# Sampling tiles of unequal width: eleven tiles of 12 columns become ten of 11, 13, 14 and 11

## The chip, the cores and the metric

The kernel runs on one core of a Trainium2 chip. A core has a matrix engine (TensorE, in the profile PE, its weight loads PEld), a vector engine (VectorE, DVE), an engine for activations and copies (ScalarE, ACT), GpSimd (POOL) and SyncE (SP), whose queue issues most DMA transfers. The metric is device time in microseconds; the median of several runs is compared.

## The reference

The input x is (2, 256, 128, 128): batch, channels, rows, columns. After a group norm, a first layer runs three branches with distances (dilations) 1, 9 and 12. Each branch computes offsets by a 3x3 convolution, samples the image at the nine shifted positions with bilinear weights, and sums the samples with one weight for each channel and tap:

```
off = conv(x, w_off, pad, dil)                   # 18 planes: (y, x) of nine taps
py = yy - pad + ky*dil + off[:, :, 0];  px = xx - pad + kx*dil + off[:, :, 1]
y  = einsum('bckhw,ck->bchw', bilinear(x, py, px), w)
out_branch = gelu(layernorm_over_channels(y))
```

The branches and a 1x1 convolution are added and normalised, a two-layer MLP with gelu follows, then a residual, a layer norm and the addition of x. A second layer adds a 3x3 convolution with weights quantised to three values. What is computed in the sampling: `sum over the four neighbours of (1-|dy|)(1-|dx|) * x`, for every tap and pixel.

## The kernel before

The program has three phases. **Phase one** (`phase_a`, up to about 0.9 ms) normalises x, writes it pixel by pixel, channels last, into a padded table in DRAM (`tables`), and computes the offsets. From these, `make_hats` writes tent functions ("hats") to DRAM: for each tap, and each of the rows and columns that a tile of source pixels has, the weight `max(0, 1 - |distance|)` that a sampling position gives to it. `offsets` also records in `reach` how far offsets go; positions that the tiles do not cover are listed by `missing` and mended singly.

**Phase two** (`sample_near`) is the sampling, and the change is in it. The padded image is cut into blocks of `RI` = 2 rows and `CI` = 12 columns; a tile of source pixels adds a margin of `REACH` = 2 on each side, so it has `TR` = 6 rows and `TC` = 16 columns, `PX` = 96 pixels, one for each partition. There are `NT` = 11 such blocks across the 132 padded columns. The outer loop goes over units: image (2), row pair `Rt` (66), branch (3). For a unit:

- `load_tiles` (L1301), once for a row pair and one row pair ahead, loads the eleven source tiles `xs`, pixel on partition, 256 channels of 4 bytes; 18 buffers turn.
- `load_hats` (L1327) loads `hy` and `hx` for each of the three tap rows: 96 partitions of 3 KB each, 2 rows by 3 taps by 128 positions. The source pattern of hy repeats the 6 row hats for each column, that of hx the 16 column hats for each row. Three buffers of each turn, so one unit fills them.
- `build` (L1347, VectorE) multiplies hy and hx into `A`, two of which turn; the positions are shifted so that a block's samples lie together.
- `sample` (L1448, TensorE) multiplies tile and A for one half of the channels: a column is one tap of one position, so a full block has 9 taps x 2 rows x 12 = 216 columns. Block 0 goes alone into a PSUM bank, then two blocks to a bank. ScalarE copies the banks to `ev` (L1460, L1468), six copies for a channel half.
- `accumulate` (L1409, VectorE; first tap L1391, ScalarE) adds the nine taps, each times its channel weight, into ring buffers of finished rows.

`columns` says which taps of a block fall inside the image. With blocks of 12 the first and last block drop three of nine taps at distance 12 and none at distance 9. A program instruction for float32 is two MATMUL records in the trace. The order on the compute engines is the program's (`pin`); between the pieces, `tail.advance` runs the rest of the network (norms, gelu, MLP) on finished groups of four rows. DMA issues are placed in SP's queue by a planner, each behind its semaphore waits, and the queue is in order: one that waits holds those behind it. `prepare(u + 2)` builds A two units ahead and asks for the hats of the unit after that.

**Phase three** (from about 5.7 ms) is the second layer's convolution.

Of the kernel before, what the change touches and what calls it, by code (L numbers as in the profile page):

```python
# [9 lines left out]
F32 = mybir.dt.float32  # L10
# [4 lines left out]
ALU = mybir.AluOpType  # L15
# [4 lines left out]
P = 128  # L20
# [20 lines left out]
RI, CI = 2, 12  # L41
TR, TC = RI + 2 * REACH, CI + 2 * REACH
NT = -(-(W + 2 * REACH) // CI)
PX = TR * TC
WT = NT * CI + 2 * REACH
AO = 12
WA = 28 + W
NH = TR + TC + 2
# [8 lines left out]
XCLS = (0, 1, 3, 9, 11)  # L57
# [3 lines left out]
SPAN = (REACH + (RI - 1) / 2, REACH + (CI - 1) / 2)  # L61
NPAT = RI + len(XCLS) + 1

# [8 lines left out]
def conv_preact_kernel(ctx: ExitStack, tc: tile.TileContext, t: dict, out: bass.AP):  # L72
# [248 lines left out]
    def phase_a(b, pool, psum, k, beside, todo):  # L321
# [53 lines left out]
        def offsets(G):  # L375
# [49 lines left out]
            nc.vector.tensor_tensor(rest, offs, k["mid"], ALU.subtract)  # L425
            planes = rest.rearrange("p r (b c k) -> p c r b k", c=2, k=9)
# [76 lines left out]
    def missing(psum, pool, tabs):  # L503
# [15 lines left out]
        nc.vector.tensor_scalar(V, reach[:, 0], SPAN[0], None, ALU.is_gt)  # L519
        nc.vector.scalar_tensor_tensor(V, reach[:, 1], SPAN[1], V, ALU.is_gt, ALU.max)  # L520
# [19 lines left out]
        for j in range(8):  # L540
            one = pool.tile([P, ROWS], F32, name="one", tag="one", bufs=3)
            nc.vector.tensor_scalar(one, slot, rank[:, j : j + 1], None, ALU.is_equal)
            nc.tensor.matmul(
                pl[0:ROWS, 0 : 2 + 2 * NTAP], lhsT=one, rhs=what[:, j, :], start=j == 0, stop=j == 7
            )
# [35 lines left out]
        nc.vector.tensor_copy(base[:, 1], pl[0:R_, 2 : 2 + 2 * NTAP])  # L581
        by, mid = base[:, :, 0:NTAP], base[:, :, NTAP:]
# [23 lines left out]
        for d in range(2):  # L606
# [3 lines left out]
            for c in range(2):  # L610
                nc.vector.tensor_scalar(cd[:, c], cd[:, c], SPAN[c] ** 2, None, ALU.is_le)
# [79 lines left out]
    def list_tables(pool):  # L691
        sizes = (NB * H + ROWS + P, NTAP, 3 * NTAP, 2 * NTAP, 8 * (2 + 2 * NTAP), NB * H)
# [15 lines left out]
    with ExitStack() as actx:  # L708
        psum = actx.enter_context(tc.tile_pool(name="ps_a", bufs=1, space=PSUM))

        def gps():
# [9 lines left out]
            "mid": ap.tile([P, ZG, NOFF], F32, name="mid"),  # L721
            "hatw": ap.tile([P, 2, NTAP * NH], BF16, name="hatw"),
# [10 lines left out]
        for b in range(NB):  # L733
# [12 lines left out]
            if b == 0:  # L746
# [3 lines left out]
                nc.sync.dma_start(k["mid"], t["mid"])  # L750
                hatw = ap.tile([P, 2, NTAP * NH], F32, name="hatw32", tag="xt", bufs=3)
# [505 lines left out]
    def sample_near(pool, psum, k):  # L1257
# [33 lines left out]
        def load_tiles(b, Rt):  # L1291

            xts[b, Rt] = []
            for T in range(NT):
                xt = pool.tile([PX, C], F32, name="xs", tag="xs", bufs=18)
                src = bass.AP(
                    table[b].tensor,
                    table[b].offset + (Rt * RI * WT + T * CI) * C,
                    [[C, TC], [WT * C, TR], [1, C]],
                )  # L1300
                nc.sync.dma_start(xt, src)  # L1301
# [109 lines left out]
        def columns(br, T):  # L1411

            dil = DILS[br]
            kept = [
                i
                for i, s in enumerate((-dil, 0, dil))
                if max(0, REACH + s) < (T + 1) * CI
                and T * CI < min(W + 2 * REACH, W + REACH + s)
            ]
            return kept[0] * RI, (kept[-1] + 1) * RI  # L1420

        def sample(u, c):
# [11 lines left out]
            n = (y1 - y0) * 3 * RI * CI  # L1434
            ev = pool.tile([P, 9 * RI, NT * CI], F32, name="ev", tag="ev", bufs=3)
            evv = ev.rearrange("p (y m) w -> p y m w", y=3)
            for T in range(-1, NT, 2):
                if T == 2 * ((NT + 1) // 4) - 1:
                    tail.advance()
                ts = range(max(T, 0), T + 2)  # L1440
                pm = k["pm"][tail.banks % len(k["pm"])]
                tail.banks += 1
                pv = pm[:, :, 0:n].rearrange("p j (y m w) -> p j y m w", y=y1 - y0, w=CI)
                reach = [columns(br, t) for t in ts]
                for j, t in enumerate(ts):
                    m0, m1 = reach[j]
                    pin(
                        nc.tensor.matmul(  # L1448
                            pv[:, j, :, m0:m1, :],
                            lhsT=xts[b, Rt][t][:, c * P : (c + 1) * P],  # L1450
                            rhs=A[:, y0:y1, m0:m1, AO + t * CI : AO + (t + 1) * CI],
# [4 lines left out]
                m0, m1 = min(r[0] for r in reach), max(r[1] for r in reach)  # L1456
                if m1 - m0 == 3 * RI:
# [512 lines left out]
```

## Time and profile before

| | |
|---|---|
| median of 3 runs | 6653.83 us (6651.51 to 6657.11) |
| profiled execution, its own time | 6654.54 us |
| its span, first to last instruction | 6652.5 us |
| mean granted TensorE clock | 0.971 |
| moved by DMA | 1360.48 MB, mean 205 GB/s |

The page gives busy time for each engine, then groups of instructions by source line: `L1448 PE MATMUL pm<-A,xs` is the sampling product of line 1448, with its count, its busy time in all and its mean duration in ns, and after the second bar the time for which the engine stood idle just before it and what ended the waiting. The chain is the work that ended last, followed back from the end; a share of it is time that the work set. In the waits, "SPq L1327 <- DVE A L1347" is a DMA issue of line 1327 that waited for the VectorE instruction that writes A.

### The profile page before, as it was taken

What the parts mean: (1) busy time and instruction counts of PE and PEld (TensorE: products, weight loads), DVE (VectorE), ACT (ScalarE), POOL (GpSimd) and SP (SyncE); (2) the same over time, 40 slices, a digit from 0 to 9 for tenths busy, and PEclk for the clock granted to TensorE, in tenths of its full rate; (3) what the DMA queues carried; (4) which work ended last, traced back from release to release, by engine and by line L of the source; (5) the groups of instructions that cost most, each with busy time, mean ns of one, the idle gap of its engine ahead of it and who ended that gap; (6) DMA issues with size and microseconds to landing.
All of it is one profiled execution on the core that took longest, in us unless ns stands there. A gap on an engine that the chain in (4) does not pass through costs nothing.

```text
span 6652.5 us, 100588 instructions
## 1 busy us (share of the span) xinstructions
PE 6295.0 (95%) x32242; PEld 5006.0 (75%) x32242; DVE 5907.6 (89%) x13772; ACT 4194.8 (63%) x8690; POOL 687.1 (10%) x665
## 2 busy tenths in 40 slices
PE   5899978999999999999999999999999999989999
PEld 3455558888888888888888888888888888734444
DVE  7766657999999999999878999999999999689996
ACT  1344436677777777777676777777777777554442
POOL 0000000111111111111110111111111111200000
PEclk9999978999999999999999999999999999989999
DMA  8976657877887777877667877778777787343332
GB/s 285 281 211 196 201 158 208 227 220 218 222 224 217 219 215 222 226 220 210 189 192 199 226 221 218 216 221 229 224 217 220 218 222 207 121 163 132 135 141 90
DMA packets 635794, 1360.48 MB, mean 205 GB/s; under 512 B 109592, under 2 KB 290344, under 8 KB 618736
## 3 DMA queue, kind: packets, MB, share of 16 engines
q1 hardware_dynamic: 617328, 1318.97, 68.8%
q10 hardware_dynamic: 17408, 33.56, 1.6%
q8 instruction: 261, 4.28, 0.3%
q14 instruction: 285, 2.33, 0.1%
q0 software_dynamic: 512, 1.34, 0.1%
HBM read 1087.10 MB, written 266.47 MB: 203 GB/s over the span
## 4 chain that ended last, share of the span: by engine, by line
PE 54%; DVE 28%; DMA 8%; ACT 6%; issue 3%; SPq 1%; POOL 0%; DVEq 0%; ACTq 0%; POOLq 0%
PE pm L1448 23%; DVE ring L1409 12%; PE hp L890 6%; PE pc L1789 6%; PE h L1133 5%; PE pz L364 4%; DVE A L1347 4%; DMA hx<-hats 3%; ACT ev L1460 3%; PE pc L1133 2%; DMA xa<-in_x 2%; ACT v L1111 2%; PE ph L463 2%; PE tp L905 1%; DVE st L1097 1%
## 5 line engine op out<-in xcount | busy, mean ns | idle before, releaser
L1448 PE MATMUL pm<-A,xs 96*128 96x216 f32 (+2 forms) x17424 | 3258.3, 344 | 180.3 <-ACT ev L1460 44.4
L1448 PEld LDWEIGHTS pm<-A,xs 96*128 96x128 f32 x17424 | 3058.0, 195 | 380.0 <-ACT ev L1460 124.2
L1409 DVE SCALAR_TENSOR_TENSOR ring<-ev,defw,ring 128x256 f32<-128x256 f32 (+4 forms) x6372 | 2481.2, 451 | 98.1 <-ACT ev L1460 52.1
L1460 ACT COPY ev<-pm 128x432 f32<-128x432 f32 (+4 forms) x4488 | 1991.9, 483 | 883.2 <-PE pm L1448 702.4
L1347 DVE TENSOR_TENSOR A<-hy,hx 96x768 f32<-96x768 f32 (+1 forms) x1124 | 1010.3, 945 | 180.3 <-DMA hx<-hats 100.2
L1103 POOL TENSOR_TENSOR rs<-rs,mhalf 128x4 f32<-128x4 f32 x320 | 472.5, 1477 | 4223.5 <-DVE rs L1102 3672.0
L1789 PE MATMUL pc<-cring,signs 128*128 128x512 bf16 x3456 | 758.2, 383 | 17.0 <-ACT cring L1706 7.4
L1111 ACT ACTIVATE v<-v,rs 128x256 f32<-128x256 f32 x1280 | 694.2, 594 | 17.0 <-POOL rs L1104 16.8
L1789 PEld LDWEIGHTS <-signs 128*128 128x128 bf16 x3456 | 339.7, 98 | 434.8 <-issue 28.0
L890 PE MATMUL hp<-S,w 128*128 128x512 f32 x1024 | 500.5, 614 | 0.8 <-ACT S L1213 0.8
L364 PE MATMUL pz<-wz,xa 128*128 128x486 f32 x1024 | 463.5, 580 | 28.1 <-DVE zr L371 28.0
L1097 DVE BATCH_NORM_STATS2 st<-v 128x6 f32<-128x256 f32 x1280 | 446.9, 410 | 35.0 <-ACT v L921 35.0
L1133 PE MATMUL h<-w,hT 128*128 128x256 f32 x2048 | 477.1, 379 | 0.0
L1391 ACT ACTIVATE ring<-ev,defw 128x256 f32<-128x256 f32 (+1 forms) x856 | 404.4, 485 | 24.1
L1133 PEld LDWEIGHTS h<-w,hT 128*128 128x128 f32 x2048 | 369.3, 190 | 65.5 <-issue 1.0
L364 PEld LDWEIGHTS pz<-wz,xa 128*128 128x128 f32 x1024 | 189.5, 192 | 193.5 <-issue 126.8
L921 ACT COPY v<-tp 128x512 f32<-128x512 f32 x384 | 207.7, 597 | 183.5 <-PE tp L913 182.7
L1222 ACT ACTIVATE hT<-hp,b 128x512 f32<-128x512 f32 x256 | 176.1, 688 | 222.5 <-PE hp L890 217.3
L890 PEld LDWEIGHTS hp<-S,w 128*128 128x128 f32 x1024 | 198.8, 199 | 141.4 <-issue 126.8
L470 ACT ACTIVATE hb<-ph 96x512 f32<-96x512 f32 (+1 forms) x384 | 209.9, 596 | 145.0 <-PE ph L463 138.6
L1133 PE MATMUL pc<-convw,xn 128*128 128x256 f32 x1024 | 271.5, 394 | 2.5 <-ACT xn L1194 2.5
L371 ACT COPY zr<-pz 128x486 f32<-128x486 f32 x128 | 72.3, 565 | 260.0 <-PE pz L364 257.3
(246 smaller groups left out, 5135.7 us busy)
## 6 DMA issues: line engine op xcount, KB each, us to landing
hy<-hats SPq DMA_DIRECT2D x1112, 288.0 KB
hx<-hats SPq DMA_DIRECT2D x1112, 288.0 KB
xs<-tables SPq DMA_DIRECT2D x1452, 96.0 KB
g12d<-v SPq DMA_DIRECT2D x128, 512.0 KB
other<-g12d SPq DMA_DIRECT2D x128, 512.0 KB
hats<-hb SPq DMA_DIRECT2D x64, 720.0 KB
hats<-hb SPq DMA_DIRECT2D x64, 576.0 KB
xa<-in_x ACTq DMA_DIRECT2D x64, 512.0 KB
```

The source lines that it names most:

```text
L364: nc.tensor.matmul(pz[:, 0:NZ], lhsT=xt[:, c, r, :], rhs=k["wz"][:, c, :], start=c == 0, stop=c == KC - 1,)
L890: nc.tensor.matmul(out, lhsT=w, rhs=v, start=i == 0, stop=i == n - 1)
L1097: pin(nc.vector.bn_stats(st[:, j, :], rows[j]))
L1103: nc.gpsimd.tensor_tensor(rs[:, 0, :], rs[:, 0, :], mhalf[:, 0:n], ALU.pow)
L1111: nc.scalar.activation(row, row, func, scale=rs[:, 0, j : j + 1], bias=rs[:, 1, j : j + 1])
L1133: nc.tensor.matmul(bank[:, j, :], lhsT=v[:, px], rhs=w, start=False, stop=i == len(pairs) - 1,)
L1347: nc.vector.tensor_tensor(dst, hy[:, i0:i1].rearrange("p i t w -> p t i w"), hx[:, i0:i1].rearrange("p i t w -> p t i w"), ALU.mult,)
L1391: pin(nc.scalar.mul(dst, src, w))
L1409: pin(nc.vector.scalar_tensor_tensor(dst, src, w, dst, ALU.mult, ALU.add))
L1448: nc.tensor.matmul(pv[:, j, :, m0:m1, :], lhsT=xts[b, Rt][t][:, c * P : (c + 1) * P], rhs=A[:, y0:y1, m0:m1, AO + t * CI : AO + (t + 1) * CI],
L1460: nc.scalar.copy(dst.rearrange("p m (t j) -> p t m j", j=CI), pm[:, 0 : len(ts), 0:n].rearrange("p t (m j) -> p t m j", j=CI),)
L1789: nc.tensor.matmul(pc, lhsT=signs[:, k, (h * 3 + t) * 3 + kx, m * P : (m + 1) * P], rhs=xc[:, i, k, t * JC : (t + 1) * JC, kx : kx + W], s ...
```

## The change

The eleven blocks of 12 columns become ten of widths 11, 13, 13, 14, 14, 14, 14, 14, 14 and 11. The borders are such that the first and last block take six of nine taps at distances 9 and 12. `columns` now also cuts positions outside the image from the first and last block, so that at distance 1 they have ten positions. `CI` is the greatest width, 14, so `TC` is 18, and the hats and A have 108 partitions; a block of n - 4 columns loads n x 6 pixels of xs (90, 102 or 108) and its product uses as many partitions. Block 0 and block 9 go alone into their PSUM banks, the others in pairs of equal width.

Positions within a block are no longer a remainder by 12: each shift of columns has its own pattern in `make_hats` (seven of them, instead of five remainders), the reach is divided by a block's own half-width (`inv`, one more VectorE multiply in each of the 32 calls of `offsets`), and the list of `missing` carries a span for each tap.

```diff
-RI, CI = 2, 12
+RI = 2
+WIDTHS = (11, 13, 13, 14, 14, 14, 14, 14, 14, 11)
+NT, CI = len(WIDTHS), max(WIDTHS)
+STARTS = tuple(sum(WIDTHS[:i]) for i in range(NT))
+WPOS = sum(WIDTHS)
 TR, TC = RI + 2 * REACH, CI + 2 * REACH
-NT = -(-(W + 2 * REACH) // CI)
 PX = TR * TC
-WT = NT * CI + 2 * REACH
-NH = TR + TC + 2
+WT = WPOS + 2 * REACH
+NH = TR + TC
...
             nc.vector.tensor_tensor(rest, offs, k["mid"], ALU.subtract)
+            nc.vector.tensor_tensor(
+                rest, rest, k["inv"].unsqueeze(1).broadcast_to([P, ZG, NOFF]), ALU.mult
+            )
...
             for T in range(NT):
+                n = WIDTHS[T] + 2 * REACH
                 xt = pool.tile([PX, C], F32, name="xs", tag="xs", bufs=18)
                 src = bass.AP(
                     table[b].tensor,
-                    table[b].offset + (Rt * RI * WT + T * CI) * C,
-                    [[C, TC], [WT * C, TR], [1, C]],
-                )
-                nc.sync.dma_start(xt, src)
+                    table[b].offset + (Rt * RI * WT + STARTS[T]) * C,
+                    [[C, n], [WT * C, TR], [1, C]],
+                )
+                nc.sync.dma_start(xt[0 : n * TR], src)
...
-            dil = DILS[br]
-            kept = [
-                i
-                for i, s in enumerate((-dil, 0, dil))
-                if max(0, REACH + s) < (T + 1) * CI
-                and T * CI < min(W + 2 * REACH, W + REACH + s)
-            ]
-            return kept[0] * RI, (kept[-1] + 1) * RI
+            p0, p1 = STARTS[T], STARTS[T] + WIDTHS[T]
+            kept, lo, hi = [], p1, p0
+            for i, s in enumerate((-DILS[br], 0, DILS[br])):
+                a, z = max(p0, 0, REACH + s), min(p1, WPOS, W + REACH + s)
+                if a < z:
+                    kept.append(i)
+                    lo, hi = min(lo, a), max(hi, z)
+            return kept[0] * RI, (kept[-1] + 1) * RI, lo, hi
...
                 for j, t in enumerate(ts):
-                    m0, m1 = reach[j]
+                    m0, m1, p0, p1 = reach[j]
+                    w = p1 - p0
+                    px = (WIDTHS[t] + 2 * REACH) * TR
+                    pv = pm[:, j, 0 : (y1 - y0) * (m1 - m0) * w].rearrange(
+                        "p (y m w) -> p y m w", y=y1 - y0, w=w
+                    )
                     pin(
                         nc.tensor.matmul(
-                            pv[:, j, :, m0:m1, :],
-                            lhsT=xts[b, Rt][t][:, c * P : (c + 1) * P],
-                            rhs=A[:, y0:y1, m0:m1, AO + t * CI : AO + (t + 1) * CI],
+                            pv,
+                            lhsT=xts[b, Rt][t][0:px, c * P : (c + 1) * P],
+                            rhs=A[0:px, y0:y1, m0:m1, AO + p0 : AO + p1],
                             start=True,
                             stop=True,
                         )
                     )
```

`load_hats` is not edited; its source patterns take `TC` and `TR` from the constants, and its tiles `PX`:

```
for h, first, dims in (
    (hy, 0, [[0, TC], [pitch, TR]]),
    (hx, TR, [[pitch, TC], [0, TR]]),
):
```

## The prediction

> **What bounds the kernel now.** I read the page first.
>
> ```profile
> PE 6295.0 (95%) x32242; PEld 5006.0 (75%) x32242; DVE 5907.6 (89%) x13772; ACT 4194.8 (63%) x8690; POOL 687.1 (10%) x665
> ...
> q1 hardware_dynamic: 617328, 1318.97, 68.8%
> ...
> PE 54%; DVE 28%; DMA 8%; ACT 6%; issue 3%; SPq 1%; POOL 0%; DVEq 0%; ACTq 0%; POOLq 0%
> PE pm L1448 23%; DVE ring L1409 12%; PE hp L890 6%; PE pc L1789 6%; PE h L1133 5%; PE pz L364 4%; DVE A L1347 4%; DMA hx<-hats 3%; ACT ev L1460 3%; PE pc L1133 2%; DMA xa<-in_x 2%; ACT v L1111 2%; PE ph L463 2%; PE tp L905 1%; DVE st L1097 1%
> ...
> L1448 PE MATMUL pm<-A,xs 96*128 96x216 f32 (+2 forms) x17424 | 3258.3, 344 | 180.3 <-ACT ev L1460 44.4
> ...
> L1347 DVE TENSOR_TENSOR A<-hy,hx 96x768 f32<-96x768 f32 (+1 forms) x1124 | 1010.3, 945 | 180.3 <-DMA hx<-hats 100.2
> ...
> hy<-hats SPq DMA_DIRECT2D x1112, 288.0 KB
> hx<-hats SPq DMA_DIRECT2D x1112, 288.0 KB
> xs<-tables SPq DMA_DIRECT2D x1452, 96.0 KB
> ```
>
> The sampling matmul is the largest share of the chain, VectorE is second, and 3% of the chain is waiting for hats to land. Next, the sampling stage alone by the windows view; it lasts from the first hats load at 916 us to the last product at 5708 us.
>
> ```profile
> 916.00:5708.00 4792.00, 4618.27 (x24775) 4114.96 (x24776) 4446.40 (x11204) 3412.61 (x7639) 656.70 (x618) 0.97 0.77 215
> ```
>
> The columns are length, busy time of PE, PEld, DVE, ACT and POOL, clock, DMA share, GB/s. TensorE is 96% busy and VectorE 93%, but the 16 DMA engines are already at 77%. They have only a factor of 1/0.77 = 1.3 in hand, and only while work is spread evenly over all 16. Then the waits of SP's queue, and the timeline of the same queue around one hats load:
>
> ```profile
> SPq L1327 <- DVE A L1347: 842.9, 493, 15.3
> SPq L1301 <- PE pm L1448: 795.5, 1012, 13.2
> ```
> ```profile
> 2356.78 0.54 SPq L1327 DMA_DIRECT2D hy<-hats  x1
> 2357.38 0.83 SPq L1327 DMA_DIRECT2D hx<-hats  x1
> ...
> 2368.19 0.55 SPq L1327 DMA_DIRECT2D hy<-hats  x1
> ```
>
> Hats loads wait until the product has freed their buffers, so unit after unit goes: product, six loads, landing, next product. Here one turn takes 2368.19 - 2356.78 = 11.4 us, while a unit takes 4792/396 = 12.1 us on average (132 row pairs by three branches). The hats turn has little slack.
>
> [...]the semaphore records of the 64 hats stores of 96 rows show their first count 2.96 us after issue, those of the 64 stores of 120 rows show one count at 0.50 us and the next at 3.60 us (k = 15), the stores of 8 rows one at 0.50 us and eight later (k = 8). [...]hy, hx and xs read 16 columns into 96 partitions, k = 16. [...]a quarter of the 3 KB packets of hats take 121 ns or less (25 GB/s), their mean with all 16 engines at work is 184 ns; xs packets of 1 KB take 46 ns at the first quarter and 58.5 ns on average.
>
> **The change part by part.**
>
> *TensorE.* Columns for one channel half and full rows: before 11 x 216 = 2376 at distances 1 and 9, and 9 x 216 + 2 x 144 = 2232 at 12; after 2 x 180 + 2 x 234 + 6 x 252 = 2340 at distance 1, and 2 x 132 + 468 + 1512 = 2244 at 9 and 12. The three branches sum to 6984 and 6828, -156. The chain has passes of 216 columns at 181 ns (14.13 us for 78), two to a product, so 1.67 ns a column. 156 x 1.67 ns x 2 halves x 132 row pairs, times 0.95 for image edges where whole tap rows drop out (1124 hats pairs of 1188), is 65 us of PE time. On the chain, PE pm is 23% of 6652 = 1550 us, of which 2.2% is 35 us. Weight loads fall by 1/11 and are hidden under the products.
>
> *ScalarE.* Six evictions before and after, slightly fewer elements (2244 to 2340 against 2304 to 2376). At 63% busy: nothing; the cover is its idle time, and without it the saving would still be a saving.
>
> *VectorE.* The product A keeps 768 elements on 108 partitions instead of 96, and its accumulations keep their shapes: zero. Each offset group in the first phase gains one multiply of 432 elements; by the zs row of that size (603 ns) 32 x 0.6 = 19 us, beside TensorE, which is 94% busy there (506.6 of 540 us) against VectorE's 71%. I take 0, and 19 if the cover is gone. The once-only list work gains three small instructions, under 1 us each.
>
> *SP's queue.* 132 fewer xs loads at 0.6 us each: 80 us of issue, off the path. With 18 buffers two tiles of the next row pair wait for the present one, where four did. One more load of constants, 27 KB, before phase one: nothing.
>
> *The transfers.* A hats load becomes 18 columns by 6 rows into 108 partitions. The largest k that divides both 18 and 108 is 9. An xs load has 18 columns for the six tiles of 14 (k = 9), 15 for the two of 11 (k = 15), and 17 into 102 for the two of 13: 17 has no divisor up to 16 but 1, so all 102 KB go through one engine, the lowest, which also serves every hats load. Its load in the stage:
> - hats: 2 x 1112 loads x 12 packets = 26,688 packets. At 121 ns 3229 us; at 184 ns 4911 us. Nine engines at 121 ns draw 228 GB/s, below the 266 GB/s that sixteen reach at 184 ns, so most of the crowding goes, but each load begins with some slow packets. I take 140 ns: 3736 us.
> - xs: per row pair 6 x 12 + 2 x 6 + 2 x 102 = 288 packets, x 132 = 38,016. At 46 ns 1749 us, at 58.5 ns 2225 us; I take 50 ns: 1901 us.
> - the rest (g12d, other, xn, xr, x1d and semaphore writes), unchanged on 16 engines: 274 us in 2 KB packets, 374 us in 4 KB packets, 46 us in counts, about 700 us.
>
> The sum is 5678, 6337 or 7836 us, against a stage of 4792 us. Before, the same engine carried 0.77 x 4792 = 3690 us. So one engine of 16 becomes the bound, with 6337 us of work that no other engine shares. Allowing 2% of gaps, 6466 us: the stage grows by 6466 - 4792 = 1674 us. The profiled run is 6654.54 us, span 6652.5 and 2.0 us around it, 0.7 us above the median of 6653.83, so the sum needs no correction: 6654.5 + 1674 = 8329, which I round to 8300. All of TensorE's 65 us vanishes under it: products wait for hats and tiles. Lower end: 5678 us with no gap, 7541. Upper: nothing eased, 9700; I do not believe that end, since nine engines cannot crowd each other as sixteen do.
>
> What is queued behind: on VectorE a late product holds the accumulations after it, these hold the ev buffers, then evictions, PSUM banks and TensorE. On SP a hats load that waits for its buffer holds back xs loads.
>
> **The rivals.**
> - *Only the nine-fold split holds; the 17-column tiles get through on many engines.* Speaks against: one rule gives both. xs then costs about 132 x (72 + 12 + 14) x 50 ns = 647 us, sum 3736 + 647 + 700 = 5083, with 5% gaps 5350: +560, 7210 (6950 to 7400).
> - *The split looks at partitions alone* (108 on 12 engines, 102 on 6). The trace cannot exclude it. Hats 26,688 x 9/12 x 140 ns = 2802, xs 132 x (6 x 9 + 2 x 17 + 2 x 6) x 50 ns = 660, rest 700: 4160 of 4792 us. That is no bound, but each load takes 9 x 150 - 6 x 184 = 250 ns longer, 1.5 us for six; at the 59 product waits 90 us, less 35 on the matmuls: 6710 (6680 to 6900).
> - *Packets spread evenly after all, and the kernel gets faster.* Then hats cost an eighth more: 1/8 of the 3.3% of the chain that waits for hx (220 us) is 27 us. Against it stand 35 us on the chain, up to 65 if VectorE follows. With 0 to 19 in phase one: 6590 to 6670, likeliest 6630. It decides only if a 108-partition load lands in no more than 7 packets an engine.
>
> **How the numbers follow.** Chances: one overloaded engine 0.84, of which 7400 to 9200 holds nearly all; nine-fold split alone 0.05; partitions alone 0.04; even spread 0.07 (0.04 faster, 0.02 within, 0.01 slower). From 7200 to 9200 takes in the first case and half of the second, just over 8 in 10. A measurement of this kernel tells about 0.2%, 13 us, from nothing; faster 0.04, same 0.02, slower 0.94.
>
> **What would show it.** Right: hx landing as the largest wait ahead of A on VectorE, hundreds to over a thousand us; the DMA share in the stage falling towards 0.5 while GB/s falls towards 170 (1032 MB and 80 MB more hats, in 6466 us); xs waits ahead of TensorE; PE busy near 70% of the stage (4618 less 65 us, of 6466); no change before 916 us and after the stage beyond 20 us. The matmul row at 15,840 instructions, 1.5 to 2% less busy by columns. Wrong: DMA share rising to about 0.85 with the stage as long as before; that would mean that the transfers use all 16 engines and the sum above has no ground.

## The result, and the profile after

The changed kernel takes 8025.48 us (median of five runs, 7997.94 to 8032.19). The kernel before, run beside it, takes 6652.32 us (6631.55 to 6657.11). The ratio is 1.206 (95% interval 1.2041 to 1.2079): 21% slower. The profiled execution took 8016.16 us with a span of 8014.4 us, at a mean granted clock of 0.901.

First the page of the changed kernel: busy time of the engines, DMA share over the span in tenths, the main DMA queue, the chain by engine and by line, and the two groups of sampling.

```profile
PE 6747.8 (84%) x30658; PEld 5037.1 (63%) x30658; DVE 5959.1 (74%) x13805; ACT 4208.2 (53%) x8690; POOL 756.1 (9%) x665
...
DMA  8867544555555555555555555555555555534332
...
q1 hardware_dynamic: 613668, 1398.09, 52.7%
...
DMA 41%; DVE 32%; PE 21%; SPq 3%; issue 2%; ACT 1%; DVEq 0%; POOL 0%; ACTq 0%; POOLq 0%
DMA hx<-hats 33%; DVE ring L1422 15%; PE pm L1465 6%; PE pc L1800 5%; DVE A L1360 5%; DMA xs<-tables 4%; PE pz L369 4%; SPq L1340 2%; DVE st L1109 2%; DMA xa<-in_x 2%; PE hp L902 1%; PE h L1145 1%; PE ph L471 1%; PE pc L1145 1%; DVE xr L1258 1%
...
L1465 PE MATMUL pm<-A,xs 108*128 108x252 f32 (+6 forms) x15840 | 3672.1, 390 | 1063.4 <-DVE A L1360 698.8
...
L1360 DVE TENSOR_TENSOR A<-hy,hx 108x768 f32<-108x768 f32 (+1 forms) x1124 | 1045.8, 951 | 1532.1 <-DMA hx<-hats 1413.7
```

Waiting for hats was 3% of the chain and is 33%; the sampling product was 23% and is 6%. At the same time the DMA row shows fives in the sampling, where the share was 0.77. So the kernel waits for transfers while the transfer engines, taken together, do less than before. That is how it would look if one engine, or a few of the sixteen, had more to do than the rest.

The sampling stage alone by the windows view, from the first product to the last (length, busy time of PE, PEld, DVE, ACT and POOL, clock, DMA share, GB/s):

```profile
936.00:7082.00 6146.00, 5075.38 (x23279) 4153.16 (x23280) 4488.66 (x11229) 3433.43 (x7664) 721.06 (x617) 0.88 0.55 181
```

The prediction's window for the kernel before ends 14 us ahead of the last product there. Counted alike, from the first hats load to the last product, the stage lasts 6152 us where it lasted 4806: 1346 of the 1362 us by which the span grew. VectorE's busy time in it rose by 34 us and ScalarE's by 13; neither is the cause. Then the waits (in us, number, longest):

```profile
DVE A L1360 <- DMA hx<-hats: 1413.7, 547, 20.8
...
PE pm L1465 <- DVE A L1360: 698.8, 143, 13.4
...
PEld pm L1465 <- DMA xs<-tables: 186.6, 66, 8.5
...
PE pm L1465 <- DMA xs<-tables: 163.1, 57, 8.1
```

The product A waited 100.2 us for hx before, and 1413.7 us after. The chain in order of time (start, length, what) shows one unit's pieces:

```profile
2493.37 12.85 DMA xs<-tables
...
2508.69 9.13 DMA hx<-hats
...
2517.91 0.96 DVE A L1360
...
2519.69 9.25 DMA hx<-hats
...
2529.03 0.96 DVE A L1360
...
2530.80 11.95 DMA hx<-hats
```

Each piece is a transfer of 9 to 13 us, with one product A of 1 us between. In the chain of before the hats pieces near 2.36 ms were 7.2 and 5.3 us long, with runs of accumulations between them.

How many engines a load used can be counted by its 4-byte packets, which are nearly all the packets under 512 bytes. The stretches in which the main queue carries only loads of one kind show what belongs to a load. Before, six hats loads (576 packets of 3 KB) come with 96 packets of 4 bytes, and for most of their time sixteen packets are under way (29 stretches); a tile load of 96 packets of 1 KB comes with 16 (65 stretches). After, a tile load of 108 packets comes with 9 (18 stretches) and one of 90 with 15 (5 stretches). I therefore take one 4-byte packet for one engine of a load. The DMA view of the stage, of before and then of after:

```profile
DMA packets 498813, 1030.20 MB, mean 215 GB/s; under 512 B 66112, under 2 KB 207808, under 8 KB 498381
```
```profile
DMA packets 495405, 1110.40 MB, mean 181 GB/s; under 512 B 38527, under 2 KB 177037, under 8 KB 494989
```

Before, 2248 hats loads and 1452 xs loads on 16 engines make 59,200, so the other transfers have 6912. After, with the prediction's k, the number of engines of a load (9 for 18 columns, 1 for 17, 15 for 15): 2248 x 9 + 792 x 9 + 264 x 1 + 264 x 15 + 6912 = 38,496, against 38,527 counted. A split by partitions alone (12, 12, 6 and 15 engines) would give 48,936, and sixteen engines for all 64,000. The count agrees with the prediction's k: 16 columns into 96 partitions 16 engines, 18 into 108 nine, 15 into 90 fifteen. 17 columns do go through one engine.

It can also be watched. In the changed kernel, from 1067.8 to 1072.7 us, nothing but xs packets runs, one behind another:

```profile
DMA packets 108, 0.11 MB, mean 22 GB/s; under 512 B 1, under 2 KB 108, under 8 KB 108
...
q1 hardware_dynamic: 108, 0.11, 6.7%
```

That is one sixteenth of the engines. Over the stage, by start and length of all packets above 4 bytes, exactly one packet is under way for 641 us (173 before), exactly nine for 2529 us, and none for 95 us; before, it was exactly sixteen for 1699 us. No record names a packet's engine, but the trace shows that the engine of the 17-column loads is one of the nine of the hats. With hats packets alone under way, exactly nine are for 1411 us of the stage and ten for 334. In the 258 stretches of at least 2 us that never have more than two xs packets under way, one xs packet with nothing but hats beside it goes with exactly eight of these for 223 us and with nine for 33. Which of the sixteen engines it is does not show; "the lowest engine", here as in the prediction and the expectations, is a name for the one that all these loads share.

### The profile page after: what moved, and what is told of

It is laid out like the page before. It is cut to its first block, busy times and chain, and to the rows that moved or that the text cites. A ratio compares the mean times of both kernels' runs of the same rounds, so it can differ in the third digit from the quotient of the medians.

```text
span 8014.4 us, 97179 instructions
## 1 busy us (share of the span) xinstructions
PE 6747.8 (84%) x30658; PEld 5037.1 (63%) x30658; DVE 5959.1 (74%) x13805; ACT 4208.2 (53%) x8690; POOL 756.1 (9%) x665
## 4 chain that ended last, share of the span: by engine, by line
DMA 41%; DVE 32%; PE 21%; SPq 3%; issue 2%; ACT 1%; DVEq 0%; POOL 0%; ACTq 0%; POOLq 0%
DMA hx<-hats 33%; DVE ring L1422 15%; PE pm L1465 6%; PE pc L1800 5%; DVE A L1360 5%; DMA xs<-tables 4%; PE pz L369 4%; SPq L1340 2%; DVE st L1109 2%; DMA xa<-in_x 2%; PE hp L902 1%; PE h L1145 1%; PE ph L471 1%; PE pc L1145 1%; DVE xr L1258 1%
## 5 line engine op out<-in xcount | busy, mean ns | idle before, releaser
L1465 PE MATMUL pm<-A,xs 108*128 108x252 f32 (+6 forms) x15840 | 3672.1, 390 | 1063.4 <-DVE A L1360 698.8
L1465 PEld LDWEIGHTS pm<-A,xs 108*128 108x128 f32 (+2 forms) x15840 | 3048.5, 211 | 1643.9 <-issue 798.0
L1477 ACT COPY ev<-pm 128x504 f32<-128x504 f32 (+5 forms) x3168 | 1753.6, 587 | 925.9 <-PE pm L1465 911.2
L1360 DVE TENSOR_TENSOR A<-hy,hx 108x768 f32<-108x768 f32 (+1 forms) x1124 | 1045.8, 951 | 1532.1 <-DMA hx<-hats 1413.7
L1483 ACT COPY ev<-pm 128x132 f32<-128x132 f32 (+4 forms) x1584 | 435.0, 275 | 1380.5 <-DVE ring L1422 1181.8
L1115 POOL TENSOR_TENSOR rs<-rs,mhalf 128x4 f32<-128x4 f32 x320 | 439.8, 1374 | 5501.8 <-DVE rs L1114 4771.3
L1116 POOL TENSOR_TENSOR rs<-rs 128x4 f32<-128x4 f32 x320 | 294.9, 922 | 25.1
```

The source lines that it names most:

```text
L1115: nc.gpsimd.tensor_tensor(rs[:, 0, :], rs[:, 0, :], mhalf[:, 0:n], ALU.pow)
L1360: nc.vector.tensor_tensor(dst, hy[:, i0:i1].rearrange("p i t w -> p t i w"), hx[:, i0:i1].rearrange("p i t w -> p t i w"), ALU.mult,)
L1465: nc.tensor.matmul(pv, lhsT=xts[b, Rt][t][0:px, c * P : (c + 1) * P], rhs=A[0:px, y0:y1, m0:m1, AO + p0 : AO + p1], start=True, stop=True,)
L1477: nc.scalar.copy(dst.rearrange("p m (t j) -> p t m j", j=w), pm[:, :, 0 : n * w].rearrange("p t (m j) -> p t m j", j=w),)
L1483: pin(nc.scalar.copy(evv[:, y0:y1, m0:m1, p0:p1], pv))
```

## The experiments

In the diffs below, "after" and "before" name the kernel that is edited. Ratios are to the kernel before, run beside each on the same chip.

**One engine, undone alone (e1).** The tiles of width 13 load 18 columns instead of 17, one of them unused; nothing else changes.

```diff
 after
-                n = WIDTHS[T] + 2 * REACH
+                n = TC if WIDTHS[T] == 13 else WIDTHS[T] + 2 * REACH
```

> The changed kernel, but the two tiles of 13 columns load 18 source columns instead of 17 (their product still uses 102 partitions, so the result is the same). By the theory of one overloaded DMA engine the load then has 9 as its common divisor instead of 1, and the lowest engine carries 8 x 12 + 2 x 6 = 108 packets of xs for a row pair instead of 288. Its work in the stage: hats 26,688 x 142 ns (the mean of their packets after the change) = 3790 us, xs 132 x 108 x 50 ns = 713, the rest 730: 5230 us, with a few per cent of gaps 5300 instead of the 6150 us that the stage now lasts: 7170 us in all (7050 to 7300), and the waits for xs ahead of TensorE almost gone. The rival that the kernel is slower because of more bytes and a longer hats turn, however the bytes are spread, expects no gain, for the loads grow by 12 KB a row pair: 8000 to 8060. The rival that the new block shapes are slow on TensorE and ScalarE expects the same.

Measured: 7197.62 us, ratio 1.0829 (1.081 to 1.0848). Loading more bytes made the kernel 828 us faster than after. Windows of its stage, its waits, and its packets:

```profile
936.00:6276.00 5340.00, 4846.14 (x23290) 3979.41 (x23290) 4477.39 (x11239) 3434.97 (x7668) 826.40 (x613) 0.94 0.62 208
```
```profile
DVE A L1360 <- DMA hx<-hats: 713.8, 386, 16.0
...
PEld pm L1465 <- DMA xs<-tables: 182.9, 46, 8.8
```
```profile
DMA packets 498204, 1110.85 MB, mean 208 GB/s; under 512 B 40536, under 2 KB 179955, under 8 KB 497788
```

With nine engines for these two tiles as well the count would be 40,608, against 40,536. The load of the lowest engine is now 26,688 hats packets at 142.6 ns (measured mean of 3 KB packets in this stage) = 3806 us, 132 x 108 xs packets at 52 ns = 741, and about 700 of the rest: 5247 of 5340 us. By this estimate the engine is full for 98% of the stage, and the stage is as long as its work. One part of the expectation missed: the waits for xs ahead of TensorE (182.9 and 165.3 us) are as long as in after. So 17-column loads are not needed for them; that xs loads of all kinds stand behind hats on nine engines would explain it, and was not tested.

e1 takes away a second thing with the first. The issue of xs loads on SP's queue, in after and in e1 (number, then shortest, median and longest in ns):

```profile
L1314 SPq DMA_DIRECT2D xs<-tables x1320: 642/771/7140, 932.9 to 7053.4; - x189
```
```profile
L1314 SPq DMA_DIRECT2D xs<-tables x1320: 737/742/1541, 926.4 to 6248.5; - x189
```

In after, the second 17-column load of a row pair holds the queue for 3.5 us on average and the load behind it for 5.0; all xs issues together take 1925 us, against 1004 in e1 and 825 before. Hats loads stand in the same queue. Whether the 828 us went through the full engine alone or also through this hold, no run separates; both come of k = 1, and some packet is under way for all but 95 us of the stage in after.

**The nine-fold split alone, in the kernel before (e2), and its control (e3).** e2 loads hats of 18 columns into 108 partitions, where only 96 are used. e3 loads 16 columns by 7 rows into 112 partitions: still more bytes, but on 16 engines. In e3 the pixels no longer stand in the order of the tile, so A gets other values; the instructions stay the same.

```diff
 before (e2; e3: 112 partitions, [[0, 16], [pitch, 7]] and [[pitch, 16], [0, 7]])
-                hy = pool.tile([PX, RI, 3, W], F32, name="hy", tag="hy", bufs=3)
+                hy = pool.tile([108, RI, 3, W], F32, name="hy", tag="hy", bufs=3)
...
-                    (hy, 0, [[0, TC], [pitch, TR]]),
-                    (hx, TR, [[pitch, TC], [0, TR]]),
+                    (hy, 0, [[0, 18], [pitch, 6]]),
+                    (hx, TR, [[pitch, 18], [0, 6]]),
...
-                    hy[:, i0:i1].rearrange("p i t w -> p t i w"),
+                    hy[0:PX, i0:i1].rearrange("p i t w -> p t i w"),
```

> The kernel before, with one thing of the change: each hats load fetches 18 columns by 6 rows into 108 partitions (324 KB), though the product still uses the first 96, so the result is the same. By the theory the load runs on 9 engines; these carry hats 26,688 x 142 ns = 3790 us, xs 132 x 66 x 55 ns = 480, the rest 730: 5000 us, with 3% of gaps 5150 against a stage of 4792: 7010 us (6850 to 7150). The rival of bytes alone expects an eighth more of the 220 us that the chain waits for hx: 6680 at most. The rival of block shapes expects 6650 to 6680, as shapes are those of before.

> The control to the run of 18 columns: the kernel before, with hats loads of 16 columns by 7 rows into 112 partitions (336 KB, more bytes than 18 by 6). 16 divides both 16 and 112, so by the theory all 16 engines take 7 packets each: 15,736 x 190 ns = 2990 us of hats, 480 of xs, 730 of the rest, 4200 of 4792 us; no bound, only longer loads: 6720 us (6660 to 6800), clearly below the run of 18 columns. The rival of bytes alone expects it at or above the run of 18 columns. The order of pixels in the hats no longer fits that of the tiles, so what is sampled is not the reference's; every instruction has the same shape as before apart from the loads.

Measured: e2 7250.06 us, ratio 1.0913 (1.0893 to 1.0934), 100 us above its range; e3 6683.73 us, ratio 1.0052 (1.0032 to 1.0072), as expected. The waits of the product in e2 and in e3:

```profile
DVE A L1347 <- DMA hx<-hats: 697.1, 358, 11.8
```
```profile
DVE A L1347 <- DMA hx<-hats: 178.4, 112, 13.3
```

The engines can be counted as above: the 2242 hats and 1441 xs loads that the DMA view of e2's stage lists give 50,146 packets with 9 and 16, against 50,201 under 512 bytes; e3 has 66,167, where 16 for every load gives 66,112. Twelve partitions more on nine engines cost 600 us; sixteen partitions more on sixteen engines cost 33 us. So it is the number of engines and not the bytes. Two things change with that number, and e2 does not part them: the work of each engine, and the issue on SP's queue, whose median for an hx load is 736 ns in e2 and 588 in e3 (587 before). All hats issues take 1684 us in e2 and 1320 in e3. The size of e2 I had too small. Its lowest engine has 26,688 x 145.6 ns = 3886 us of hats, 132 x 11 x 6 = 8712 xs packets at 57.6 ns = 502, and 700: 5088 us, 95% of its stage of 5378 us. In e1 the share was 98%. What keeps the engine idle for the other 5% was not settled; that hats loads wait for the product of the unit before may leave it dry at times.

**Twelve blocks of 11 (e4).** Every load has 15 columns and 90 partitions, the shape that ran on 15 engines in after (15 packets of 4 bytes to a load). This should have kept the gain in columns without the loss.

```diff
 after
-WIDTHS = (11, 13, 13, 14, 14, 14, 14, 14, 14, 11)
+WIDTHS = (11,) * 12
...
-                if T == NT // 2:
+                if T == 5:
```

> The changed kernel with twelve blocks of 11 columns instead of ten of unequal width (and the step of the rest of the network after the same bank as before). First and last block again take 6 of 9 taps at distances 9 and 12 and ten columns at distance 1, so the columns that TensorE processes are the same 6828 of 6984 for three branches. A load has 15 columns by 6 rows, 90 partitions: 15 engines, 6 packets each, as many per engine as before. By the theory the overload is gone and TensorE's saving is left: 35 us on the chain, up to 65: 6590 to 6650, likeliest 6620. There are 7 evictions for a channel half instead of 6, about 3000 ns in sum against 2950, hidden. The rival of block shapes (edge blocks alone in a bank, changed evictions) expects a kernel slower than before, above 6700.

Measured: 6926.8 us, ratio 1.0426 (1.0406 to 1.0446), 277 us above the range. The wait of A for hx is 320.5 us, against 1413.7 in after and 100.2 before, so transfers were no longer what mainly held it, and the count by columns had to be looked at. The groups of the sampling product by form, full rows, before and in e4:

```profile
L1448 PE MATMUL pm<-A,xs 96*128 96x216 f32 x14304 | 2852.9, 353 | 132.8 <-ACT S L1213 41.9 <-ACT ev L1460 28.6 <-issue 22.1
```
```profile
L1465 PE MATMUL pm<-A,xs 90*128 90x198 f32 x13760 | 2823.0, 358 | 48.3 <-ACT ev L1483 48.0
```

A MATMUL record of 198 columns takes 358 ns on average, one of 216 columns 353 ns. The columns do not set the time alone. I therefore took the distance from one matmul's start to the next from the traces, tile by tile (medians in ns, steady part):

```
kernel  width  AO + start, remainder by 4    distance
before   12     0                            182
after    13     0, 3                         199
after    14     1                            212
after    14     3                            246
e4       11     0, 1                         167
e4       11     2, 3                         185
```

A product reads from A windows of w positions: 18 windows, one for each tap and row. In this table the product is slower where such a window touches one more aligned group of four float32 than its width needs: 14 positions from remainder 3 touch five groups (246 ns), from remainder 1 four (212 ns); 11 positions from remainder 2 or 3 touch four (185 ns), from 0 or 1 three (167 ns). Three of the six 14-wide blocks of the change stand at remainder 3. What makes these windows slower the traces do not show.

With these distances, three branches and one channel half make 2 x 11 x 182 + 9 x 182 + 2 x 122 = 5886 ns before. After, the sum is 6068 ns: 3.1% more where the prediction had 2.2% less. With AO = 13, one position further, no 14-wide window touches a fifth group, and the sum is 5784 ns, 1.7% less than before. For both halves, two records to a product, 132 row pairs, and the prediction's 0.95: +91 us and -51 us. For e4 the same sum gives some 110 of the 276 us by which it is slower than before. The rest stays open; one rival is SP's queue, where a hats load on 15 engines takes 0.82 us to issue and all hats loads 1866 us, against 1316 before.

**The same transfers with the windows shifted (e7).**

```diff
 after
-AO = 12
+AO = 13
```

> The changed kernel with AO = 13 alone, transfers as in the change. By the theory of one overloaded DMA engine TensorE is not the bound, so the time stays within 30 us of 8025 although the three slow tiles of 14 fall from 246 to 212 ns a pass. A theory that puts the slowdown on slower products expects several hundred us of gain.

Measured: 8019.3 us, ratio 1.2058 (1.2026 to 1.2089), the same as after within its interval. The groups of 252 columns in after and in e7:

```profile
L1465 PE MATMUL pm<-A,xs 108*128 108x252 f32 x8256 | 2281.4, 421 | 158.3 <-DMA xs<-tables 146.3 <-ACT ev L1483 11.7
```
```profile
L1465 PE MATMUL pm<-A,xs 108*128 108x252 f32 x8256 | 2157.5, 406 | 182.8 <-DMA xs<-tables 162.1 <-ACT ev L1483 20.0
```

TensorE's largest group became 124 us shorter and the kernel did not become faster: TensorE is not what bounds the changed kernel.

**Without the last two columns (e8, e9).** Loads of 16 columns and 96 partitions ran on 16 engines before (16 packets of 4 bytes to a load); here the hats loads and eight of the ten tiles have this shape. The samples that lie in the two columns left out are missing from the output (two unused hat rows keep the stores of phase one as they were); the products have 96 partitions in place of 108 and 102, and the same columns. e9 shifts the windows as well.

```diff
 after
-TR, TC = RI + 2 * REACH, CI + 2 * REACH
+TR, TC = RI + 2 * REACH, 16
-NH = TR + TC
+NH = TR + TC + 2
...
-                n = WIDTHS[T] + 2 * REACH
+                n = min(WIDTHS[T] + 2 * REACH, TC)
...
-                    px = (WIDTHS[t] + 2 * REACH) * TR
+                    px = min(WIDTHS[t] + 2 * REACH, TC) * TR
 e9 also
-AO = 12
+AO = 13
```

> The changed kernel with the last two of 18 source columns left out of every hats load and tile: 16 columns by 6 rows, 96 partitions, 16 engines, the same bytes a hats load as before, the same number of issues on SP as the change, and the block widths, products, evictions and sums of the change (products on 96 instead of 108 partitions). What samples take from those two columns is left out of the result. This is the change with its transfers out of the way. By columns, as predicted, TensorE's saving of 35 to 65 us is left: 6590 to 6650. By the pitch seen in the traces (passes of three branches 6068 against 5886 ns, +96 us in all) it is slower than before: 6690 to 6760. Above 6900 something else in the change costs time that neither the transfers nor the pitch explain.

> The run before it with the margin AO of A at 13 elements instead of 12; the same part of the result is left out. The tiles of 14 then all run at 212 ns a pass, the passes of three branches sum to 5784 ns, 102 less than before the change, 54 us in all: 6600 to 6650, and 70 to 150 us below the run with 12. If the pitch in a kernel that TensorE bounds does not matter as it does in the sum, the two are within 30 us.

Measured: e8 6686.01 us, ratio 1.0055 (1.0037 to 1.0073); e9 6613.17 us, ratio 0.995 (0.9933 to 0.9967). The stage of e8 by windows, then the sampling product of e8 and of e9:

```profile
927.00:5752.00 4825.00, 4665.73 (x23252) 3854.94 (x23252) 4454.07 (x11228) 3415.88 (x7659) 667.85 (x613) 0.98 0.75 210
```
```profile
L1465 PE MATMUL pm<-A,xs 96*128 96x252 f32 (+6 forms) x15840 | 3326.5, 365 | 173.4 <-ACT S L1225 48.9
```
```profile
L1465 PE MATMUL pm<-A,xs 96*128 96x252 f32 (+6 forms) x15840 | 3174.1, 354 | 228.9 <-ACT ev L1477 81.9
```

All that the change does apart from the last two columns leaves the kernel at 6686 us; 1339 of the 1373 us hang on these two columns, which set k. With the transfers out of the way the windows do show: the product is busy 68 us longer in e8 than before (3258.3 us), and e9 is 152 us below e8, where the distances give 91 + 51 = 142. The kernel gets 73 us of that. By columns alone e8 should have been faster than before, and it is not.

**The loads in two parts (e5, e6).** To keep all 18 columns, 16 of them load on 16 engines and the other two in a load of their own, row first, on six engines: e5 has 19,824 more packets under 512 bytes than e8, six for each of its 3304 loads of two columns. All go through SP's queue. e6 shifts the windows as well.

```diff
 after (hats; the tiles xs are split in the same way)
-                    (hy, 0, [[0, TC], [pitch, TR]]),
-                    (hx, TR, [[pitch, TC], [0, TR]]),
+                    (hy, 0, [[0, 16], [pitch, TR]], 0, 16 * TR),
+                    (hx, TR, [[pitch, 16], [0, TR]], 0, 16 * TR),
+                    (hy, 0, [[pitch, TR], [0, 2]], 16 * TR, PX),
+                    (hx, TR + 16, [[0, TR], [pitch, 2]], 16 * TR, PX),
 e6 also
-AO = 12
+AO = 13
```

> The changed kernel with every load of more than 16 columns in two: 16 columns by 6 rows into 96 partitions (16 engines, 6 packets), and the last two columns, ordered row first, 6 by 2 into 12 partitions (6 engines, 2 packets); tiles of 13 take a column of zeros as their eighteenth, so the result is the same. By the theory the lowest engine now carries hats 2 x 1112 x 8 packets x 170 ns = 3020 us, xs 132 x 76 x 55 ns = 550, the rest 730: 4300 us, no bound, and the 1370 us go away. What TensorE then does is open. The prediction by columns expects 6590 to 6650. The pitch of the products in the traces says otherwise: in the changed kernel three of the six tiles of 14 take 246 ns a pass and three 212, so that the passes of three branches sum to 6068 ns against 5886 before, +3.1%, 96 us in all: 6690 to 6760. A third rival is SP's queue: 12 hats issues and 6 of xs for a unit at 0.6 us, with the rest 11.4 of 12.1 us: if it is the bound, 6800 to 7000 with waits for hx and xs.

> The run before it with one number changed: the margin AO ahead of position 0 in a row of A is 13 elements instead of 12, so that each tile of 14 begins at an offset of 0 or 2 modulo 4 and its 14 float32 touch four groups of four, never five. If the slow passes come from windows that touch one group of four more than needed, all six tiles of 14 take 212 ns, the passes of three branches sum to 5784 ns against 5886 before (-1.7%, 54 us in all), and the kernel is 60 to 150 us faster than with 12: 6590 to 6650. If the pitch goes by columns alone, or by something else in these tiles, it is within 10 us of the run with 12. If SP's queue is the bound, both are the same, 6800 to 7000.

Measured: e5 8270.41 us, ratio 1.2426 (1.2398 to 1.2455); e6 8230.44 us, ratio 1.2386 (1.2362 to 1.2409). Both are slower than the changed kernel and beyond every case that I had named. The timeline of SP's queue in e6 (start, length, issue) points to the reason; the first two issues are loads of 96 partitions, the last two of 12:

```profile
3000.83 0.59 SPq L1350 DMA_DIRECT2D hy<-hats  x1
3001.46 0.59 SPq L1350 DMA_DIRECT2D hx<-hats  x1
3002.09 0.74 SPq L1350 DMA_DIRECT2D hy<-hats  x1
3002.88 0.73 SPq L1350 DMA_DIRECT2D hx<-hats  x1
```

The issues stand without a gap, and a load of 12 partitions costs SP more time than one of 96: 0.74 against 0.59 us. All hats issues of the stage take 3003 us in e6 and 1316 before, 1688 us more in the turn "product, loads, landing, product", and e6 is 1577 us slower than before. Other loads of this queue come late as well: the network's xn is waited for 689.3 us, 1.5 us before. The sum fits, but the issues of xs take 788 us more besides, which must have found room in SP's waits; what else adds to it was not tested apart.

**The rest on GpSimd's queue (e12).** The 16 columns go through SP, the last two of the hats through GpSimd, the 13-wide tiles load 18 columns, and AO is 13.

```diff
 after (with AO = 13 and the edit of e1)
-                    (hy, 0, [[0, TC], [pitch, TR]]),
-                    (hx, TR, [[pitch, TC], [0, TR]]),
+                    (nc.sync, hy, 0, [[0, 16], [pitch, TR]], 0, 16 * TR),
+                    (nc.sync, hx, TR, [[pitch, 16], [0, TR]], 0, 16 * TR),
+                    (nc.gpsimd, hy, 0, [[0, 2], [pitch, TR]], 16 * TR, PX),
+                    (nc.gpsimd, hx, TR + 16, [[pitch, 2], [0, TR]], 16 * TR, PX),
```

> The changed kernel, result complete, with AO = 13 and the hats loads in two: 16 columns on SP's queue (16 engines) and the last two columns, 12 partitions, on GpSimd's queue, which takes six of these for a unit. Tiles of 13 load 18 columns (9 engines), so SP has as many issues as in the change. The lowest engine carries 36 packets of hats and 36 of xs for a unit and a small share of the rest: 10.2 of 12.1 us. If GpSimd's queue takes its six loads in its idle time (it is 10% busy), the kernel comes near the run with the two columns left out (6613) plus three quarters of the 33 us that a sixth more bytes cost the control: 6640 (6610 to 6690). If its loads wait behind the norms' instructions in order, or the norms behind them, 6750 to 7300.

Measured: 7034.0 us, ratio 1.0576 (1.0551 to 1.0601): better than after, worse than before, and in the second of the expected cases. Two lines of its waits:

```profile
POOL hy L1342 <- DVE A L1362: 1363.3, 336, 15.2
...
SPq L1342 <- DMA hy<-hats: 415.1, 96, 9.2
```

GpSimd now stands 1363.3 us at hats loads that wait for their buffers, and SP waits for the part that GpSimd loads. The expectation's reason, norms that wait behind these loads, fits; how much of the time each of these costs was not measured.

**Twelve blocks that stand well (e10, e11).** With these widths the windows of the first ten blocks touch no more groups than they need, and tiles of 16 columns give the hats loads the shape of before, which ran on 16 engines. e11 also keeps 24 rows of hats for each tap.

```diff
 after
-WIDTHS = (11, 13, 13, 14, 14, 14, 14, 14, 14, 11)
+WIDTHS = (11,) + (12,) * 8 + (7, 7, 11)
-AO = 12
+AO = 13
...
-                if T == NT // 2:
+                if T == 5:
 e11 also
-NH = TR + TC
+NH = TR + TC + 2
```

> Complete result. Twelve blocks of 11, eight of 12, 7, 7 and 11, with AO = 13, so that every block of 12 begins at a multiple of four: 16 columns, 96 partitions, 16 engines. By the pitches seen (152, 182, 105 and about 139 ns; 112 to 123 at the edges) the passes of three branches sum to about 5875 ns, as before (5886). If the 270 us by which twelve blocks of 11 were slow come from the products' alignment and what follows from it, this kernel takes 6640 to 6720. If twelve blocks are slow in themselves (seven evictions and twelve tile loads instead of six and eleven), it takes 6850 to 6950 again.

> The run of twelve aligned blocks with two more, unused, hat rows for a tap (NH 24 instead of 22), as the kernel before has them. With 22 the hats stores of phase one have 88 and 110 rows, of which 11 is the largest divisor up to 16, and phase one ended 92 us later (first product at 1022 us against 930); with 24 they have 96 and 120 rows, 16 and 15 engines. By the theory of divisors the first product comes at 930 us again and the run takes 6745 us (6720 to 6770). If the late start has another cause, 6820 to 6850.

Measured: e10 6834.75 us, ratio 1.0278 (1.0258 to 1.0298), between the two expected cases; e11 6743.8 us, ratio 1.014 (1.0115 to 1.0166), as expected. In e10 the first product of the sampling starts at 1013 us of the span; in e11 at 924, as in before (920). (The expectation gives the same starts some 10 us later, from another zero.) With 22 rows for a tap the hats stores of phase one have 88 and 110 rows, with 24 they have 96 and 120; in before a store of 96 rows comes with 16 packets of 4 bytes and one of 120 with 15. How many engines the stores of 88 and 110 rows use was not counted. That e10's second loss of 91 us is the same thing in another place is therefore an estimate of mine; e11, which differs from e10 in these rows alone, fits it. The stage of e11:

```profile
933.00:5808.00 4875.00, 4685.10 (x26422) 4204.22 (x26421) 4456.70 (x11230) 3505.67 (x8450) 640.68 (x611) 0.96 0.75 212
```

It is 83 us longer than before, with transfers at the same share and TensorE busy 67 us more. The twelfth block brings a seventh eviction (ScalarE 93 us more), further tile loads and weight loads; which of these costs the time stays open. The distances do not: summed as above they make about 5880 ns, as before.

No version that loads and uses all columns was faster than the kernel before.

## Why the prediction was right, and where it was off

**What became the bound: right.** One engine of sixteen as the limit fits what was measured: the counts of 4-byte packets give k = 9, 1 and 15 to 0.1%, e1 removes k = 1 and gains 828 us, e2 shows k = 9 alone at +600 us, and e3 shows that the bytes are worth 33. The two parts together come close to the whole: 828 us for the one engine and 600 for the nine make 1428, against 1373. What the runs show is that k sets the time; how much of it goes through full engines and how much through the longer issues on SP's queue stays open. All three rivals fall: "nine-fold only" at 7210 us describes e1 (7198 us) very well, but it is not what the change does; "partitions alone" falls by the count; "even spread" falls by the count too, and by the DMA share of 0.55. Beforehand k was an estimate of mine from the divisors of a load's columns and partitions: of before, the stores of 96, 120 and 8 rows had shown 16, 15 and 8 engines.

**The size: stage +1346 us where +1674 was forecast**, an end of 8025 us in place of 8300. Hats were taken at 140 ns a packet, and the stage's mean is 142.5. So that term, 26,688 x 142.5 ns = 3803 us, was right to 2%. With xs and the rest as forecast the lowest engine would have 3803 + 1901 + 700 = 6404 us to do, in a stage that lasts 6152. The price of xs was too high: where its packets run one behind another with no other under way, they start 45.3 ns apart on average, not 50 (16,909 cases in the trace), which makes 38,016 x 45.3 ns = 1722 us. That leaves 627 us for the rest and the gaps, where 829 had been put. So the gaps or the rest were too large as well; since no record names a packet's engine, the trace does not tell which. The price of hats, taken by judgement between 121 and 184 ns, came out right, and that is in part luck.

**VectorE, ScalarE, phase one and the end: right.** The first product starts at 936 us instead of 920, within the 0 to 19 us given for the multiply. But e3, without the multiply, has 936 and e8, with it, 920, so the runs show no price for it. From the last product to the end it is 931 us before and 932 after. VectorE's product has a mean of 951 ns on 108 partitions and 945 on 96.

**The signs to look for.** hx is the largest wait ahead of A (1413.7 us), the DMA share fell to 0.55 ("towards 0.5"), GB/s to 181 ("towards 170"), and TensorE waits 350 us for xs, where its matmuls waited 19.1 us before. These hold, though in e1 the last of them is as long without any 17-column load.

**The step that failed: TensorE's columns.** "1.67 ns a column", so 65 us less, has the wrong sign. The price of a column was right (0.84 ns in each of the two records) for windows that stand well. Windows of 14 that touch a fifth group of four cost 34 ns more in each record, and the sum is 91 us more. (On the way, 23% of 6652 us is 1530 and not 1550; the 35 us are 34.) In this kernel it did not matter for the time (e7), since TensorE waits. But the rival "even spread", at 6630 us and faster, rested on it; e8, even without the two columns' bytes, shows 6686 us in its place. With AO = 13, e9's 6613 us and three quarters of e3's 33 us (12.5% instead of 16.7% more bytes of hats) (25 us) would make about 6638 us, an estimate: hardly a gain even where transfers spread evenly.

**SP's queue: put at nothing, and not nothing.** The prediction has 80 us less of xs issue, "off the path", and nothing on the issue of hats. In the trace xs issues grow from 825 to 1925 us, by the 17-column loads, and hats issues from 1316 to 1676, since one takes 0.74 instead of 0.55 to 0.59 us. e6 suggests that time on this queue can be paid in full.

**PE's busy share: wrong.** I gave "near 70%" of the stage and it is 5075.38 / 6146 = 83%, and the matmul row is busy 3672.1 us, not 1.5 to 2% less than 3258.3. A TensorE that waits did not simply have the same busy time in a longer stage: its granted clock was 0.88 there, against 0.97 before. The clock records have two values, 0.5 and 1.0, and change in steps of 3.4 us; at 0.5 the kernel before spends 384 us, the changed one 1590. In the 3.4 us ahead of the 205 stretches at 0.5 TensorE had been busy for 30% of the time, ahead of those at 1.0 for all of it (medians). At 0.5 records of 252 columns start 420 ns apart, at 1.0 212 or 246. Of the 414 us by which the matmul row grew, e8 shows 68 with the transfers out of the way. Of the changed kernel's product records 2151 ran wholly at 0.5, 602 before, which makes some 300 us more, an estimate; the remainder stays open.

## What to carry to other kernels

When a tile size is changed, count on how many DMA engines each load of the new shape runs, as here by its 4-byte packets: two tiles of 17 columns cost 828 us, more than all the rest of the change, and loading one unused column more won that back. Here a matmul's time followed its column count only where the windows that it reads touched as few groups of four float32 as they can; try a shift of the data or other borders (e8 to e9: one number, 73 us). And splitting a load into a good and a small part was no way out where the queue that issues them lies in the turn: each small load cost more to issue than a large one.

## What the runs showed that I had not expected

- 252 columns in windows of 14: 212 ns from start to start with windows from remainder 1 by four, 246 ns from remainder 3; 198 columns in windows of 11: 167 or 185 ns. So 198 columns could cost more than 216 in windows of 12 (182 ns).
- Half clock for 1590 us of the changed kernel against 384 us before, with waits of up to 20.8 us spread over the stage.
- Issue of one hats load on SP's queue: 0.55 to 0.59 us for 96 partitions (before) and 112 (e3), 0.74 for 108 on nine engines (after, e2), 0.82 for 90 on fifteen (e4), 0.74 for 12 (e6). Whatever its size, a hats load on fewer than sixteen engines took longer.
- 3 KB packets on nine engines took 142.5 ns, on sixteen 184.3 ns. What the nine lose in number they win back in part, and GB/s fell by 16% only (215 to 181).
